# Images 3 and 4 convolved in 4x4 tiles, statistics as sums and squares on ScalarE, copies of the image in the linear attention

## The chip, the cores and the metric

One core of a Trainium2 chip runs the whole kernel. The metric is the device time of one execution in microseconds (us); the kernel before takes 3007.32 us (median of three runs, 3005.36 to 3007.85). All data are 32-bit floats. In the profile PE is TensorE, the matrix engine (PEld its weight loads), DVE is VectorE, ACT is ScalarE, POOL is GpSimd, and SP is the engine that issues most DMAs. Each of them works through its own list of instructions in the order written, and waits on semaphores where an operand or a buffer belongs to another.

## The reference

Four images of 256 channels and 64x64 pixels pass through four residual layers. Each layer first normalises its input by groups (`_gn`), so each needs the mean and variance of the whole image that the layer before it has just made.

```python
x = x + L0(_gn(x))   # 3x3 convolution, group norm, ReLU; non-local attention; 1x1; group norm
x = x + L1(_gn(x))   # RMS norm, linear attention in 4 heads, RMS norm
x = x + L2(_gn(x))   # dynamic depthwise 3x3 and pointwise convolution, kernels from pooled features
x = x + L3(_gn(x))   # mixture of 4 experts as one 1x1 convolution

# layer 0
xs = conv3x3(x, smooth_w) + smooth_b
xs = relu(group_norm(xs))                      # 8 groups
f  = einsum('bnc,bcm->bnm', theta_x, phi_x)    # 4096 x 4096 for each image
y  = einsum('bnm,bmc->bnc', softmax(f), g_x)
return group_norm(conv1x1(y, w_w)) * 0.1 + xs
```

## The kernel before

**Stages.** The image is kept as 128 partitions (channels of one half) by two halves by 4096 pixels. Image 1 is convolved alone (`convolve_first`) and projected to theta, phi and g (`project`). Then there is one stage for each image's non-local attention. `attend(b)` is a generator of 128 steps: a step multiplies 1024 columns of logits (`pf`, line 1021), takes their exponential on ScalarE (`pr`, line 1022), multiplies the step's probabilities with g (`py`, line 1129) and adds them up on VectorE (`tot`). The logits of a step are issued one step ahead of the products that use them. Every 16 steps a block of 512 rows ends, and its normalisation and output projection (`ended_by_dram`, lines 1038 to 1080) follow inside the next steps.

**What runs beside it.** `run(Chain(...).steps(), attention)` interleaves a second stream with these steps. The second stream is a generator that yields amounts of work; `Chain` multiplies them by a rate and lets one attention step go by for each whole unit (`steps`). `w.later(n, f)` puts a function n steps later. So a yield of 0.62 at a rate of 0.83 spaces the work by 0.51 attention steps. Beside the attention of image 1 (b = 0) run `scale_weights`, `filters_across` and `convolve_second`, at rate 1.33. Beside that of image 2 and of image 3 run `tail` of the image before and `convolve` of the image after, at rate 0.83. Beside image 4's runs the tail of image 3 at 1.2. After each stage comes `project`, which has the matrix engine to itself; the tail of image 4 is last and alone. Below, "stage 2" and "stage 3" are the attentions of images 2 and 3.

**The tail** of an image is `nonlocal_out` (normalise the attention's output, add it to the image; the sums of line 135 and statistics at line 1242), `linear_attention` (statistics at line 1431), `generated` (normalise, depthwise taps on VectorE, pointwise products on PE at line 1577, statistics at line 1591) and `mixed` (experts, line 1804).

**Two forms of the convolution.** Both turn the 3x3 convolution into products of transformed tiles, with the filters transformed once and kept in DRAM (`rows_d`, `filters`). `convolve` (images 3 and 4) makes 4x2 output tiles: 6x4 = 24 products for a tile, each product four matmuls of 512 columns, 96 matmuls in all. `convolve_second` (image 2) makes 4x4 output tiles: 36 products taken as 18 pairs, each pair eight matmuls of 256 columns, 144 matmuls in all (line 601). Its input is laid out by column phase (`planar`), written in `normalise_planar` (lines 661 on VectorE and 663 on ScalarE); `convolve` normalises in place (lines 670 and 672). Each product needs a tile `v` that VectorE makes from the row transform `ra` (`down` and `across`); the results are joined on VectorE from PSUM. A product's matmuls are put one step after its `v`. At the end the ReLU pieces run, two at once and the others inside `project`: one ScalarE instruction of 1024 columns for each piece after `convolve` (line 703), four of 256 columns with a re-ordering after `convolve_second` (line 698).

**Statistics.** They come from `bn_stats` on VectorE (512 columns at a time), except in the tail of image 4, where the pointwise result uses a sum taken by the adding instruction itself (line 1593) and squares on ScalarE with an accumulator (line 1595).

**Loads and copies.** The filter tiles `u` come through ScalarE's queue in `convolve` and through SP's in `convolve_second`. `copy_x` copies the raw image from DRAM to DRAM (`xs_d`) during the convolution. While `convolve` runs, the DMA that turns the row sums (`turning`, line 1054) goes through SP, else through ScalarE's queue.

## Time and profile before

The profiled execution took 3005.05 us, with a span of 3003.3 us from its first to its last instruction, so it lies 2 us under the median of the runs; 2 us of it lie outside the span.

| stretch of the span, us | what runs | length |
|---|---|---|
| 0 to 181 | image 1: convolution, projection | 181 |
| 181 to 744 | attention 1, convolution of image 2, projection | 563 |
| 744 to 1467 | attention 2, tail 1, convolution of image 3, projection | 723 |
| 1467 to 2190 | attention 3, tail 2, convolution of image 4, projection | 723 |
| 2190 to 2749 | attention 4, tail 3 | 559 |
| 2749 to 3003 | rest of attention 4, tail 4 | 255 |

A row of the group view reads: line, engine, operation, tiles written and read, partitions by elements, count, then busy time, mean duration of one in ns, and the engine's idle time before these instructions with what ended it. One matmul of the program is two matmul instructions in the profile (a 32-bit product is made in two passes), so the 96 matmuls of one image's convolution are 192 there and the 144 of the other form are 288. Instructions of one engine overlap at their ends: the spacing of two that follow each other is less than the duration of one.

### The profile page before, as it was taken

To read this page: it belongs to the slowest core of one execution; us is meant where nothing else is said; L and a number is where in the kernel's file an instruction comes from. 1 tells how busy PE (TensorE), PEld (TensorE's weight loads), DVE (VectorE), ACT (ScalarE), POOL (GpSimd) and SP (SyncE) were. 2 spreads that over 40 slices of the span, in tenths; PEclk is the share of its full clock that TensorE was granted. 3 is DMA by queue.
4 is the path that set the end of the run, shared out by engine and by line. 5 is a ranking of instruction groups with operands and counts; after the bars stand their busy time and mean duration, and the time that the engine had idled before them with its cause. 6 is when DMAs were issued, how large, how long until landed. Compare 5 with 4: busy or idle time off the path is not lost.

```text
span 3003.3 us, 25088 instructions
## 1 busy us (share of the span) xinstructions
PE 2953.0 (98%) x8750; PEld 1511.7 (50%) x8750; DVE 2058.4 (69%) x2835; ACT 1192.8 (40%) x2318; POOL 132.3 (4%) x182
## 2 busy tenths in 40 slices
PE   7999999999999999999999999999999999999998
PEld 3454555555565444444566444444546644444744
DVE  8747667773646994778455797578655468886585
ACT  2234333335456333322455533412335454333732
POOL 0000000001001000000001000000000100000100
PEclk9999999999999999999999999999999999999999
DMA  5245534224402225431610334243431222244021
GB/s 225 76 98 114 60 60 77 39 35 100 90 4 36 32 25 140 86 72 35 161 8 11 53 20 88 78 88 67 89 101 14 25 42 46 28 95 91 22 70 68
DMA packets 536133, 200.58 MB, mean 67 GB/s; under 512 B 471040, under 2 KB 481024, under 8 KB 532480
## 3 DMA queue, kind: packets, MB, share of 16 engines
q1 hardware_dynamic: 127808, 163.25, 17.6%
q10 hardware_dynamic: 403584, 18.88, 12.0%
q0 software_dynamic: 4608, 16.78, 3.7%
q8 instruction: 71, 1.16, 0.2%
q14 instruction: 62, 0.51, 0.1%
HBM read 130.13 MB, written 85.52 MB: 72 GB/s over the span
## 4 chain that ended last, share of the span: by engine, by line
PE 81%; DVE 12%; issue 5%; ACT 1%; POOL 0%; DMA 0%; DVEq 0%; POOLq 0%; ACTq 0%
PE pf L1021 25%; PE py L1129 24%; PE ps_conv L529 5%; PE ps_tp L957 4%; PE ps_qk L1303 3%; PE ps_ex L1804 3%; PE ps_pw L1577 3%; DVE tot L132 2%; DVE dw L135 2%; PE ps_conv L601 2%; PE ps_ctx L1330 2%; PE ps_g L962 2%; PE ps_o L1399 2%; PE ps_wy L1073 2%; PE ps_dw L1624 1%
## 5 line engine op out<-in xcount | busy, mean ns | idle before, releaser
L1022 ACT ACTIVATE pr<-pf 128x512 f32<-128x512 f32 x1024 | 603.1, 596 | 1092.0 <-PE pf L1021 1034.3
L1021 PE MATMUL pf<-tpg 128*128 128x512 f32 x2048 | 966.3, 594 | 0.0
L1129 PE MATMUL py<-pr,tpg 128*128 128x512 f32 x2048 | 961.7, 592 | 0.0
L132 DVE TENSOR_TENSOR tot<-tot,pr 128x1024 f32<-128x1024 f32 x448 | 546.5, 1220 | 181.8 <-ACT pr L1022 181.0
L1129 PEld LDWEIGHTS py<-pr,tpg 128*128 128x128 f32 x2048 | 389.2, 190 | 489.7 <-issue 481.6
L1021 PEld LDWEIGHTS pf<-tpg 128*128 128x128 f32 x2048 | 383.0, 190 | 428.4 <-issue 407.3
L135 DVE SCALAR_TENSOR_TENSOR dw<-xp,dk,dw 128x1008 f32<-128x1008 f32 x208 | 263.1, 1268 | 6.7 <-ACT dw L1569 3.6
L529 PE MATMUL ps_conv<-v,u 128*128 128x512 f32 x384 | 170.9, 593 | 3.2 <-DVE v L132 3.2
L132 DVE TENSOR_TENSOR tpg<-ps_g,bg_s 128x512 f32<-128x512 f32 x32 | 22.1, 692 | 146.9 <-PE ps_g L962 146.9
L529 PEld LDWEIGHTS ps_conv<-v,u 128*128 128x128 f32 x384 | 72.8, 190 | 95.8 <-issue 89.1
L957 PE MATMUL ps_tp<-big,wtpg_s 128*128 128x512 f32 x256 | 116.3, 594 | 2.7 <-ACT big L698 2.0
L225 POOL TENSOR_TENSOR rstd<-rstd,half 128x2 f32<-128x2 f32 x24 | 17.5, 729 | 2194.4 <-DVE rstd L382 2070.5
L1303 PE MATMUL ps_qk<-wqkv_s,xg 128*128 128x256 f32 x496 | 113.1, 379 | 0.0
L1303 PEld LDWEIGHTS ps_qk<-wqkv_s,xg 128*128 128x128 f32 x496 | 94.0, 190 | 21.3 <-issue 8.6
L1577 PE MATMUL ps_pw<-dw,pk 128*128 128x512 f32 x216 | 98.0, 593 | 0.9 <-DVE dw L135 0.9
L958 ACT ACTIVATE tpg<-ps_tp,btp_s 128x512 f32<-128x512 f32 x64 | 44.0, 687 | 95.3 <-PE ps_tp L957 95.3
L957 PEld LDWEIGHTS ps_tp<-big,wtpg_s 128*128 128x128 f32 x256 | 46.6, 190 | 54.5 <-issue 45.2
L1313 ACT ACTIVATE qk<-ps_qk,rinv 128x256 f32<-128x256 f32 x100 | 46.9, 474 | 65.2 <-PE ps_qk L1303 62.9
L962 PEld LDWEIGHTS ps_g<-wtpg_s,big 128*128 128x128 f32 x512 | 62.2, 192 | 15.3 <-issue 15.3
L132 DVE TENSOR_TENSOR v<-ra 128x1024 f32<-128x1024 f32 x58 | 69.2, 1221 | 0.3
L1812 ACT ACTIVATE res<-ps_ex,b 128x512 f32<-128x512 f32 x56 | 38.2, 687 | 76.0 <-PE ps_ex L1804 72.4
L1577 PEld LDWEIGHTS ps_pw<-dw,pk 128*128 128x128 f32 x216 | 40.9, 190 | 53.2 <-issue 49.7
(391 smaller groups left out, 3099.0 us busy)
## 6 DMA issues: line engine op xcount, KB each, us to landing
xp<-in_x_dram SPq DMA_DIRECT2D x16, 1024.0 KB, 8.1
xs_d<-big POOLq DMA_DIRECT2D x32, 512.0 KB, 6.4
wy_d<-wt SPq DMA_DIRECT2D x32, 512.0 KB, 2.8
wy<-wy_d SPq DMA_DIRECT2D x32, 512.0 KB, 4.0
out_dram<-res SPq DMA_DIRECT2D x64, 256.0 KB, 2.0
xs_d<-in_x_dram SPq DMA_DIRECT2D x24, 512.0 KB, 6.0
xs<-xs_d SPq DMA_DIRECT2D x24, 512.0 KB, 4.7
wp<-in_wp_dram SPq DMA_DIRECT2D x16, 512.0 KB, 5.3
```

The costliest lines, as they stand in the source:

```text
L132: nc.vector.tensor_tensor(o, a, b, op)
L135: nc.vector.scalar_tensor_tensor(o, a, s, b, op0, op1)
L529: nc.tensor.matmul(ps[oh], u(oh, h), v[:, bass.ts(h, 512)], start=(h == 0), stop=(h == NH - 1))
L601: nc.tensor.matmul(ps[:, bass.ts(oh, IY * IX)], u[i][:, h, bass.ts(oh, P)], v[:, i, bass.ts(h, IY * IX)], start=(h == 0), stop=(h == NH - 1))
L957: nc.tensor.matmul(ps, wtpg_s[:, h, k, :], big[:, h, cols], start=(h == 0), stop=(h == NH - 1))
L962: nc.tensor.matmul(ps[:, j, :], big[:, h, bass.ts(4 * c + j, P)], wtpg_s[:, h, 2, :], start=(h == 0), stop=(h == NH - 1))
L1021: nc.tensor.matmul(pf, phi[:, bass.ts(2 * m + s, P)], theta[:, bass.ts(q, 512)], start=True, stop=True)
L1022: nc.scalar.activation(pr[:, bass.ts(s, 512)], pf, AF.Exp)
L1129: nc.tensor.matmul(py, g[:, bass.ts(2 * m + s, P)], probs[i][:, bass.ts(s, 512)], start=(m == 0 and s == 0), stop=(m == NM - 1 and s == 1))
L1303: nc.tensor.matmul(ps[:, 0:2 * HID], xg[:, h, bass.ts(j, P)], wqkv_s[:, h, 0:2 * HID], start=(h == 0), stop=(h == NH - 1))
L1577: nc.tensor.matmul(ps, pk[:, h * NH * P + oh * P:h * NH * P + (oh + 1) * P], dw[h][:, bass.ts(s, 512)], start=(h == 0), stop=(h == NH - 1))
L1804: nc.tensor.matmul(ps, wm[h][:, bass.ts(oh, P)], big[:, h, bass.ts(c, 512)], start=(h == 0), stop=(h == NH - 1))
```

## The change

Images 3 and 4 are convolved by the same function as image 2, now called `convolve(w, b, pace)`. The old `convolve` is gone. The statistics of `nonlocal_out`, of the 4x4 convolution and of `generated` are taken as sums and squares: the sums by VectorE's adding instruction or by ScalarE, the squares by ScalarE. The last few lines of moments that this needs were in two places and are now two functions. `copy_x` for images 3 and 4 is issued in the linear attention's loop, and all filter tiles come through SP's queue.

```diff
+    def sums_tile():
+        return sp.tile([P, 2, NH, N // 512], F32, name="sums", bufs=1)
+    def joined_moments(st, sums, minus):
...
+    def accumulated(sums, pivot, parts=N // 512):
...
+    def load_filter_of(us, i, n):
+        if i < len(PRODUCTS):
+            a, pair = PRODUCTS[i]
+            k = pair[n]
+            u = filter_tile("u")
+            nc.sync.dma_start(out=u, in_=rows_d[...] if k in (0, 5) else filters[a, :, k - 1])
+            us.append(u)
@@ planar_joiner
+        def sums_of(n):
+            k, oh, s = 1 + n // 4, n // 2 % 2, n % 2
+            for i, f in enumerate((AF.Identity, AF.Square)):
+                nc.scalar.activation(junk()..., outs[:, oh, k, bass.ts(s, 2), :], f,
+                                     bias=minus[:, oh:oh + 1], accum_out=sums[...])
@@ input_stats
-                yield 0.3
+                yield 0.2
@@ normalise_planar
-            yield 1
+            yield 0.6
@@ normed_relu
-            if b == 1:
+            if b > 0:
@@ convolve
-    def convolve(w, b):
...
-    def convolve_second(w):
+    def convolve(w, b, pace):
+        us = []
+        if b > 1:
+            for n in range(2):
+                load_filter_of(us, 0, n)
         _, gm, rstd = yield from input_stats()
         yield from normalise_planar(gm, rstd)
...
-                for j in range(3):
-                    w.later(5 + j, lambda j=j: stats(j))
+                w.later(5, lambda: stats(0))
+                for j in range(8):
+                    w.later(6 + j, lambda j=j: sums_of(j))
...
-                pace = 1.8 if a == 5 else 0.87
+                slow = (2.07 if a == 5 else 1) * pace
                 for op, *args in down(a, planar, ra, rt, ra):
                     op(*args)
-                    yield 0.75 * pace
+                    yield 0.75 * slow
...
             for op, *args in ops:
                 op(*args)
-                yield 0.4 * pace
+                yield 0.4 * slow
             w.later(1, lambda ...: multiply(a, pair, v, u, after))
-            yield pace
+            yield slow
@@ ended_by_dram
-            turning[0].dma_start(...)
+            nc.scalar.dma_start(...)
...
             tt(yt, yt, inv, ALU.mult)
+            yield
             yield
@@ nonlocal_out
+        def squares(c, h):
+            for s in range(2):
+                nc.scalar.activation(junk(), big[:, h, bass.ts(2 * c + s, 512)], AF.Square, bias=about[:, h:h + 1],
+                                     accum_out=sums[:, 1, h, 2 * c + s:2 * c + s + 1])
         for i, (c, h) in enumerate(PARTS):
-            added(i, sc)
+            added(i, sc, accum_out=sums[:, 0, h, c:c + 1])
...
-            yield 0.7
-            for s in range(2):
-                nc.vector.bn_stats(st[:, h, 2 * c + s, :], big[:, h, bass.ts(2 * c + s, 512)])
-            yield 0.7
+            w.later(1, lambda c=c, h=h: squares(c, h))
+            yield 0.9
         w.settle()
+        yield from w.pending()
@@ linear_attention, loop over c
+            elif b + 2 < B and c % 2 == 0:
+                copy_x(b + 2, c // 2)
@@ generated, pointwise_added
-                    tt(big[:, oh, cols], res[oh], big[:, oh, cols], ALU.add)
-                    nc.vector.bn_stats(st[:, oh, c, :], big[:, oh, cols])
+                nc.vector.scalar_tensor_tensor(big[:, oh, cols], res[oh], 1.0, big[:, oh, cols], ..., accum_out=...)
+            def squares():
+                for oh in range(NH):
+                    nc.scalar.activation(junk(), big[:, oh, cols], AF.Square, bias=pivot[...], accum_out=...)
+            if diag is None:
+                w.later(1, squares)
@@ the stages
-            parts = [tail(b - 1, big, qT), lambda w: convolve(w, b + 1)] if b > 0 else [
-                scale_weights, filters_across, convolve_second]
+            parts = [tail(b - 1, big, qT), lambda w: convolve(w, b + 1, 0.53)] if b > 0 else [
+                scale_weights, filters_across, lambda w: convolve(w, 1, 0.87)]
-            run(Chain(both(*parts), 1.33 if b == 0 else 0.83).steps(), attention)
+            run(Chain(both(*parts), 1.365 if b == 0 else 0.775).steps(), attention)
-        run(Chain(tail(B - 2, big, qT, held=held), 1.2).steps(), attention)
+        run(Chain(tail(B - 2, big, qT, held=held), 1.225).steps(), attention)
```

By the order of the changed program, one image of stages 2 and 3 has its first convolution product in attention step 88 and its last in step 115, where it was 97 and 118. The tail is over, and `normalise_planar` runs, by step 84 to 87. In both programs the second stream ends within the 128 steps.

## The prediction

> **What bounds the kernel now.** I read first the page's span and busy times, which say that PE is busy for all but 50 us:

> ```profile
> span 3003.3 us, 25088 instructions
> ...
> PE 2953.0 (98%) x8750; PEld 1511.7 (50%) x8750; DVE 2058.4 (69%) x2835; ACT 1192.8 (40%) x2318; POOL 132.3 (4%) x182
> ```

> Next came windows by stage (PE, PEld, DVE, ACT, POOL busy, clock, DMA). The first two rows are stage 2, up to and from its first convolution product. The third is image 2's convolution, in the form that images 3 and 4 are to get. The last two are projections, after the old form and after the 4x4 form.

> ```profile
> 743.70:1230.50 486.80, 483.42 (x1435) 247.40 (x1434) 339.67 (x477) 218.95 (x449) 25.42 (x32) 1.00 0.28 53
> 1230.50:1390.00 159.50, 159.50 (x372) 70.78 (x373) 129.51 (x140) 34.89 (x59) 0.00 (x0) 1.00 0.39 73
> ...
> 329.00:670.00 341.00, 341.00 (x939) 178.14 (x939) 239.86 (x285) 109.60 (x185) 0.00 (x0) 1.00 0.36 57
> ...
> 1422.00:1466.80 44.80, 44.80 (x201) 27.79 (x200) 9.99 (x11) 19.54 (x26) 5.17 (x6) 1.00 0.69 142
> 696.00:743.70 47.70, 45.67 (x200) 27.50 (x199) 9.99 (x11) 27.74 (x44) 5.17 (x6) 1.00 0.63 127
> ```

> PE is full at clock 1.00, so PE work removed is time gained, as long as nothing makes PE wait. In 159.5 us of the old convolution VectorE has 30 us to spare. The 4x4 form of image 2 had 341 us for its VectorE work, and 101 to spare. The view of PE's waits over stage 2 shows how little it waits now:

> ```profile
> PE ps_conv L529 <- DVE v L132: 1.6, 1, 1.6
> PE ps_wy L1073 <- DVE yq L132: 1.1, 1, 1.1
> PE pm L364 <- DVE mv L132: 0.8, 2, 0.6
> ```

> The groups view prices the pieces:

> ```profile
> L529 PE MATMUL ps_conv<-v,u 128*128 128x512 f32 x384 | 170.9, 593 | 3.2 <-DVE v L132 3.2
> L601 PE MATMUL ps_conv<-v,u 128*128 128x256 f32 x288 | 65.1, 379 | 0.0
> L672 ACT ACTIVATE xp<-xp,nb,rstd 128x1024 f32<-128x1024 f32 x12 | 14.1, 1232 | 1.6 <-DVE nb L135 1.6
> L1595 ACT ACTIVATE junk<-tpg,pivot 128x512 f32<-128x512 f32 x16 | 11.6, 723 | 5.8 <-DVE tpg L1593 5.4
> L663 ACT ACTIVATE big<-xp,nb,rstd 128x1024 f32<-128x1024 f32 x4 | 9.1, 2286 | 2.4 <-DVE nb L135 2.4
> ```

> The timeline gives the spacing of instructions that follow each other, which is what counts where an engine is full:

> ```profile
> 668.92 2.35 DVE L132 TENSOR_TENSOR xp<-xp,rt 128x1024 f32<-128x1024 f32 x2
> ...
> 670.38 1.88 PE L1129 MATMUL py<-pr,tpg 128*128 128x512 f32 x4
> ...
> 672.10 1.88 PE L1021 MATMUL pf<-tpg 128*128 128x512 f32 x4
> ```
> ```profile
> 644.87 2.50 DVE L135 SCALAR_TENSOR_TENSOR rt<-sums 128x512 f32<-128x512 f32 x4
> ```
> ```profile
> 587.40 1.28 DVE L135 SCALAR_TENSOR_TENSOR ra<-big 128x1088 f32<-128x1088 f32 x1
> 588.60 1.22 DVE L132 TENSOR_TENSOR tot<-tot,pr 128x1024 f32<-128x1024 f32 x1
> ```

> Four matmuls of 512 columns take 1.72 us (0.43 each), so an attention step is 3.44 us of PE. On VectorE 512 elements cost (2.50-0.69)/3 = 0.60 us (0.69 is their duration alone), 1024 cost 2.35-1.22 = 1.13 and 1088 cost 1.20.

> **The change, part by part.** All terms are us in one execution.

> 1. *Matmuls.* Old, for one image: 170.9/2 = 85.4. New: 288 instructions, 65.1. Saved 20.3 an image, 40.7 for two. L601 costs 65.1/288 = 0.226 each against 170.9/384 = 0.445: half the columns, half the time. [...]

> 2. *The convolution against VectorE.* In the changed order, from first to last product of an image (28 steps), PE has 288 conv instructions (65.1), 216 of attention (0.43: 92.9) and 8 of output projection (3.4): 161. VectorE has 127 operations of 512 elements (76.2), 51 of 1024 (57.6), 20 of 1088 (24.0), small ones 2, and about 30 that read what the one before wrote, 0.1 more each: 163. The spare 30 us are gone: VectorE can't be ahead, each product's `v` becomes ready late, and behind it on PE wait the next logits, their exponentials and the next `tot`. At least the 2 us of excess and some 3 for the first `v`, which comes after the normalisation, are lost: 5. At most VectorE overlaps nothing: by full durations (0.69, 1.22, 1.285) its sum is 181, 20 more than PE, with the first `v` 23. VectorE must also wait for each product before it joins it, several short waits. I take 10, nearer the back-to-back rows, as VectorE will run back to back.

> 3. *Planar normalisation on ScalarE.* Four passes of L663 (2.29) take the place of four of L672 (1.23), in 2.4 x 0.775 = 1.9 steps, 6.4 us. ScalarE has 9.1 and two steps' exponentials (four of 0.6 overlapping, 2.2): 11.3, 4.9 too many. The exponentials wait in the queue behind the passes and `py` behind them; cover is the lead of one step. Range 0 to 5; I take 3.8. [...]

> 4. *Squares of `nonlocal_out`.* Sixteen of L1595's kind, 0.72 and some 0.13 for reading the accumulator (the 256-wide squares of L1285 last 0.38 and stand 0.51 apart): 13.6, within 8 x 0.9 x 0.775 = 5.6 steps or 19.2 us, beside 6.0 of exponentials: full. Each square waits for VectorE's addition, exponentials queue behind it. From 0 (one step's lead covers) to 7 (two pieces' four squares, 3.4, in a heap, twice): 4. The `bn_stats` saved on VectorE there (16 of 0.60) are off the path.

> 5. *Tail squeezed.* Rate 0.775 for 0.83: a tap (1.18 on VectorE) with its share of `tot` needs 1.18 + 0.48 x 1.13 = 1.72 in 0.62 x 0.775 = 0.48 steps, 1.65 of PE; it was 1.76 in 1.77. Over 64 taps VectorE falls 4.5 behind unless the pointwise products (64 instructions, 27.5) give it time. Other hand-overs in the tail lose cover alike. 0 to 10: 5. The pointwise statistics moved to ScalarE cost nothing there: by the first window it is busy 219 of 487.

> 6. *ReLU pieces.* The projection after the planar form is 47.7-44.8 = 2.9 longer: 2.9 an image (2 to 4).

> 7. *Removed waits:* 1.6 and about 0.9 of the others, -2.5.

> 8. *Stage 1.* `sums_of` (16 x 0.85) follows VectorE's joins for a = 4, exponentials queue behind: 0 to 5, taken 2.5. Last stages 0 (-2 to 2).

> 9. *DMAs.* SP's queue gets 36 filter loads an image and loses the turning DMA; ScalarE's loses 24 loads. A filter's second tile is loaded after the product before, 1.7 + 3.44 + 1.7 us ahead of use, and lands in 3.1 (median in the DMA view): hidden; 0. `copy_x` moves to another stretch with DMA share 0.28: 0.

> Sum: -40.7 + 2 x (10 + 3.8 + 4 + 5 + 2.9 - 2.5) + 2.5 = +8.2. On the profiled 3005.05 that is 3013.3; the median before is 2.3 above it: **3015**. The change breaks even where the stalls of a stage (25.7 here) come to 21.6.

> **The rivals.**

> *The cover holds.* Exponentials issued a step ahead and the buffers absorb all but 5 + 2.9 a stage: -40.7 + 2 x (7.9 - 2.5) = -29.9, 2977. For it: image 2's planar form in this trace made PE wait for nothing between 329 and 670. Against: there a product had 2.8 times the steps, and VectorE 101 us to spare. Half way to my stalls is 2996.

> *VectorE is the bound at full durations.* Term 2 at 23, the others as taken: +26 and +8.2 = +34, 3041. For it: dependent operations hardly overlap. Against: the back-to-back rows.

> *Filters late.* If SP's longer queue makes a tile land in 8 us rather than 3.1, 1.1 is lost in each of 36 products: +40, 3055. Against: stage 1 has this load order and no such wait.

> *It doesn't do what it says:* excluded for PE's work, since the changed order has 144 more matmuls of 256 columns in place of 96 for each image.

> **How the numbers follow.** 0.2% (6 us) is about what a measurement can tell from none. My forecast, stalls of 20 to 32 a stage, has 0.55: 0.39 slower, 0.15 within 6 us, 0.01 faster. The cover holds 0.25 (0.21 faster, 0.04 same). VectorE as bound 0.13, filters 0.07: slower but for 0.01. Together 0.22 faster, 0.20 same, 0.58 slower. My own case spans 3004 to 3028; the range reaches to 2988 and 3034, which leaves about 0.1 out on each side.

> **What would show it.** Conv matmuls of both stages near 130 us in all; PE's waits with ps_conv behind DVE `v`, about 10 in each of stages 2 and 3 and VectorE over 95% busy there; `py` behind ACT `pr` during the squares and the planar passes; projections of 47 to 48. I am wrong if PE waits less than 15 us a stage, or if its waits name a DMA.

## The result, and the profile after

The changed kernel takes 3029.24 us (median of four runs, 3025.12 to 3031.41) against 3007.26 (3005.36 to 3007.85): a ratio of 1.0073, 95% interval 1.0055 to 1.0090. It is 22 us slower. The profiled execution took 3028.17 us with a span of 3025.8.

The page's first lines:

```profile
span 3025.8 us, 26129 instructions
...
PE 2933.2 (97%) x8942; PEld 1558.0 (51%) x8942; DVE 2055.9 (68%) x2979; ACT 1330.3 (44%) x2654; POOL 131.6 (4%) x184
```

PE is busy 20 us less than before, half of what the matmuls were to save, and the span is 22.5 longer. Where: by the first logits of each attention, stage 1 grew from 562.6 to 565.2 us, stage 2 from 723.1 to 731.6, stage 3 from 723.1 to 733.5, and the rest from 813.3 to 813.8.

PE's waits in stage 2 (engine, line, what it waited for; us in all, times, longest):

```profile
PE ps_conv L658 <- issue: 7.2, 2, 4.5
PE py L1098 <- ACT pr L990: 7.1, 4, 3.1
PE ps_pw L1548 <- DVE dw L135: 2.5, 1, 2.5
PE ps_tp L927 <- ACT big L755: 2.0, 3, 0.7
PE ps_conv L658 <- DVE v L132: 1.8, 1, 1.8
PE ps_zt L1412 <- DVE zr L1389: 1.7, 2, 1.5
PE ps_b L1477 <- DVE w1n L132: 1.4, 1, 1.4
```

These are the stalls that were forecast, nearly to the microsecond: 9.0 for the convolution (the profile finds no releaser for two of its three waits and says "issue"), 7.1 for `py` behind ScalarE, and the tail's hand-overs. The longest "issue" ends as the first of VectorE's two operations on `v`, 0.69 long, does (start, length, engine, line, operation; in brackets the wait before it):

```profile
1369.02 1.41 DVE L135 SCALAR_TENSOR_TENSOR v<-v 128x512 f32<-128x512 f32 x2
1369.80 6.36 PE L658 MATMUL ps_conv<-v,u 128*128 128x256 f32 x16 [4.47 <-issue]
```

All of PE's idle time in stage 2 went from 4.0 to 24.8 us, in stage 3 from 4.1 to 26.0.

The surprise is in the column of the clock. Windows of the changed kernel, the stretch of the convolution and then five short ones around its longest wait (length, PE, PEld, DVE, ACT, POOL busy, granted clock, DMA share, GB/s):

```profile
1213.90:1388.00 174.10, 165.11 (x517) 100.87 (x516) 165.82 (x208) 46.58 (x81) 0.00 (x0) 0.97 0.35 65
```
```profile
1361.56:1364.97 3.41, 3.41 (x9) 1.33 (x7) 3.38 (x5) 1.78 (x3) 0.00 (x0) 1.00 0.00 0
1364.97:1368.38 3.41, 0.36 (x1) 0.00 (x0) 3.37 (x4) 0.00 (x0) 0.00 (x0) 1.00 0.44 84
1368.38:1371.80 3.42, 2.00 (x5) 1.67 (x6) 3.32 (x7) 0.00 (x0) 0.00 (x0) 0.50 1.30 37
1371.80:1375.21 3.41, 3.41 (x10) 2.69 (x9) 3.34 (x8) 0.60 (x1) 0.00 (x0) 0.50 1.87 28
1375.21:1378.62 3.41, 3.41 (x12) 1.87 (x11) 2.90 (x5) 1.30 (x3) 0.00 (x0) 1.00 1.00 84
```

PE does 0.36 us of work in the second window; in the next two its clock is 0.50, and then 1.00 again. VectorE is busy throughout, so it is the engine that PE waits for. In the kernel before, the clock was 1.00 in all of stages 2 and 3; here 27.3 us of them lie at 0.50, each time at or just after one of the longest waits. The convolution's matmul instructions follow each other at 0.427 us there (the median of 37) and at 0.216 elsewhere. PE is busy 25.2 of these 27.3 us, so 12.6 us are lost to it. This is the part that the prediction lacks.

### The profile page after: what moved, and what is told of

It is laid out like the page before. It is cut to its first block, busy times and chain, and to the rows that moved or that the text cites. A ratio compares the mean times of both kernels' runs of the same rounds, so it can differ in the third digit from the quotient of the medians.

```text
span 3025.8 us, 26129 instructions
## 1 busy us (share of the span) xinstructions
PE 2933.2 (97%) x8942; PEld 1558.0 (51%) x8942; DVE 2055.9 (68%) x2979; ACT 1330.3 (44%) x2654; POOL 131.6 (4%) x184
## 3 DMA queue, kind: packets, MB, share of 16 engines
q8 instruction: 72, 1.18, 0.2%
## 4 chain that ended last, share of the span: by engine, by line
PE 85%; DVE 8%; ACT 3%; issue 2%; DMA 1%; POOL 0%; SPq 0%; DVEq 0%; POOLq 0%; ACTq 0%
PE pf L989 26%; PE py L1098 26%; PE ps_conv L658 6%; PE ps_tp L927 3%; PE ps_qk L1284 3%; PE ps_pw L1548 3%; PE ps_ex L1779 3%; PE ps_ctx L1311 2%; PE ps_wy L1042 1%; PE ps_dw L1599 1%; PE ps_row L611 1%; PE ps_conv L572 1%; PE ps_g L932 1%; PE ps_o L1382 1%; DVE dw L135 1%
## 5 line engine op out<-in xcount | busy, mean ns | idle before, releaser
L132 DVE TENSOR_TENSOR tot<-tot,pr 128x1024 f32<-128x1024 f32 x448 | 546.7, 1220 | 191.0 <-ACT pr L990 189.7
L135 DVE SCALAR_TENSOR_TENSOR dw<-xp,dk,dw 128x1008 f32<-128x1008 f32 x208 | 263.1, 1269 | 6.7 <-ACT dw L1540 3.6
L658 PE MATMUL ps_conv<-v,u 128*128 128x256 f32 x864 | 205.0, 392 | 19.2 <-issue 14.4
L658 PEld LDWEIGHTS ps_conv<-v,u 128*128 128x128 f32 x864 | 170.0, 197 | 69.6 <-issue 36.7
L132 DVE TENSOR_TENSOR tpg<-ps_g,bg_s 128x512 f32<-128x512 f32 x32 | 22.1, 692 | 153.1 <-PE ps_g L932 153.1
L135 DVE SCALAR_TENSOR_TENSOR sums<-ps_conv,sums 128x512 f32<-128x512 f32 x72 | 49.7, 690 | 51.1 <-PE ps_conv L658 49.9
L663 ACT ACTIVATE sums<-ps_conv 128x512 f32<-128x512 f32 x36 | 21.5, 598 | 118.1 <-PE ps_conv L658 118.1
L1787 ACT ACTIVATE res<-ps_ex,b 128x512 f32<-128x512 f32 x56 | 38.2, 688 | 73.4 <-PE ps_ex L1779 70.6
```

What stands on the lines that cost most here:

```text
L132: nc.vector.tensor_tensor(o, a, b, op)
L135: nc.vector.scalar_tensor_tensor(o, a, s, b, op0, op1)
L658: nc.tensor.matmul(ps[:, bass.ts(oh, IY * IX)], u[i][:, h, bass.ts(oh, P)], v[:, i, bass.ts(h, IY * IX)], start=(h == 0), stop=(h == NH - 1))
```

## The experiments

**1. Filling the waits** (stall and clock told apart).

```diff
+    def busy(ps, n):
+        for i in range(n):
+            nc.tensor.matmul(ps[:, 0:P], ones, ident, start=(i == 0), stop=(i == n - 1))
@@ multiply, logits, pointwise_products (stages 2 and 3)
+    busy(...)   # 5, 9, 17 before three products; 11 before one pair of logits; 8 before one pointwise product
```

> The changed kernel, and besides in each of stages 2 and 3 short matmuls that no result depends on (ones by the identity, 128 columns, some 0.22 us each; their bank is overwritten at once by the product behind them), put on PE just ahead of the five longest waits: 11 (2.4 us) where the planar normalisation makes `py` wait 3.1, 5 (1.1) in the convolution's wait of 1.8, 9 (2.0) in that of 2.7, 17 (3.7) in that of 4.5, 8 (1.7) in the pointwise products' wait of 2.5. The waits' ends are set by ScalarE and VectorE, so the fillers lie inside them. Theory (half clock): PE runs at half speed for 3.4 or 6.8 us after a wait that left it idle for most of a 3.4 us window; 27.3 us at 0.5 in stages 2 and 3 cost half of that, 13.7. With the fillers these rows of 0.5 are gone and the time is 3029.2 - 13.7 = 3015.5 (3012 to 3018), with the same waits of ps_conv, py and ps_pw less the fillers. Rival (the waits are all of it; the recorded half clock costs nothing, or comes from something else than idle time): 3029 (3027 to 3032), or the rows of 0.5 stay.

Measured: 3018.62 us (3017.09 to 3019.11), ratio to before 1.0039 (1.0026 to 1.0053): 10.6 less than the changed kernel, by adding work, and 0.6 above the range of the theory. Only one window at half clock is left in stages 2 and 3 (behind the squares of stage 3, which had no filler). PE's waits in stage 2:

```profile
PE py L1106 <- ACT pr L998: 4.7, 4, 2.2
PE ps_conv L664 <- DVE v L132: 2.9, 4, 1.2
...
PE ps_pw L1558 <- DVE dw L135: 0.7, 1, 0.7
```

The same waits, less the fillers. Half of the busy time at half clock fell from 12.6 to 1.7, so 10.9 were to be had (the 13.7 of the theory counted the windows' whole length, and all of them); stages 2 and 3 became 9.4 shorter and the span 10.9. The rival falls.

**2. What triggers the half clock.** The kernel before, with waits of set length in stage 1.

```diff
+            if b == 0 and i in IDLE:          # every 7 steps, 1 to 7 copies, twice
+                t = junk()
+                for s in range(2):
+                    ps = bank("ps_idle")
+                    nc.tensor.matmul(ps, ones, theta[:, 0:512] if s == 0 else t, start=True, stop=True)
+                    for j in range(IDLE[i] if s == 0 else 0):
+                        nc.scalar.copy(t, ps if j == 0 else t)
```

> The kernel before with 14 waits put into the attention of stage 1, where PE is full: every 7 steps one matmul, a chain of 1 to 7 ScalarE copies of 512 columns (some 0.5 us each) that starts from its result, and a matmul that reads the chain's end; nothing uses the results. PE is idle some 0.8 to 4.5 us each time, twice for each length. Theory (a free-running grid of windows of 3.413 us; one in which PE is idle for more than about 0.6 halves the clock of the next): waits under 2 us are never followed by 0.5, waits over 4.1 always, and between them it goes by the share of the window and not by the length: every window above 0.65 idle is followed by 0.5, none below 0.55; all starts of 0.5 lie on one grid of 3.413 us. Rival (the length of the wait decides, from about 2.5 us): waits of 2.5 to 4 are all followed by 0.5, wherever they fall.

Measured (one execution, 3091.72 us): waits of 0.68, 1.38 and 1.98 us were never followed by 0.50; those of 3.01, 3.27, 3.98 and 4.57 always. Two waits of nearly one length went different ways. Windows on the grid around the wait that ended at 339.8 (2.68 us) and around that at 593.0 (2.63 us):

```profile
334.53:337.94 3.41, 2.57 (x6) 0.78 (x5) 2.79 (x4) 1.91 (x4) 0.00 (x0) 1.00 0.57 107
337.94:341.35 3.41, 1.58 (x4) 0.86 (x5) 0.19 (x1) 1.72 (x3) 0.00 (x0) 1.00 0.06 22
341.35:344.77 3.42, 3.42 (x9) 1.51 (x9) 0.00 (x0) 1.00 (x2) 0.00 (x0) 1.00 0.00 0
...
590.53:593.95 3.42, 0.94 (x2) 0.49 (x3) 2.03 (x2) 2.34 (x4) 0.00 (x0) 1.00 0.00 0
593.95:597.36 3.41, 3.41 (x5) 1.35 (x4) 0.00 (x0) 0.00 (x0) 0.00 (x0) 0.50 0.00 0
597.36:600.77 3.41, 3.41 (x9) 1.52 (x8) 0.83 (x1) 1.19 (x2) 0.00 (x0) 1.00 0.00 0
```

**3. Spacing the planar normalisation.**

```diff
-            yield 0.6
+            yield 0.6 if b == 1 else 1.2
```

> The changed kernel with 1.2 in place of 0.6 between the four quarters of the planar normalisation of images 3 and 4 (1.9 attention steps more for it, and the convolution two steps later). Theory: four passes of 2.25 us then share 3.7 steps with the exponentials and fit; the 3.1 us wait of `py` falls to 1.5 or less, and with it one halved window, so at least 2 x (1.6 + 1.7) = 6.6 go: 3022.6, and less, down to 3005, if the convolution's waits of 2.7 and 4.5 (which fall differently against the ends of the blocks of 16 steps) come under 2 us too and their halved windows go as well. Rival (the wait only moves: VectorE is full behind it anyway, and what the normalisation gives is lost in the convolution): 3027 to 3031.

Measured: 3011.29 us (3008.55 to 3013.35), ratio 1.0016 (1.0007 to 1.0025), 18 less than the changed kernel. The wait of `py` fell from 3.1 to 1.0; the convolution's waits of 2.7 and 4.5 became 1.6, 1.3 and 1.6, and the windows at 0.50 there are gone. That lies between the two values expected, and the rival falls: PE's idle time in the two stages went from 50.8 to 41.7.

**4. VectorE's load in the convolution.**

```diff
-            elif m > 1:
+            elif m > 1 and not (b in (1, 2) and 88 <= i < 116):
                 tt(tot, tot, probs[i], ALU.add)
```

> The changed kernel without VectorE's `tot` additions in steps 88 to 115 of stages 2 and 3 (26 additions of 1024 columns a stage, 29 us; the row sums are then short of these steps). Theory (the convolution's waits come from a full VectorE that brings `v` late): with 29 us less of 166 VectorE is ahead, the conv waits of 9.0 and 11.2 us fall under 2 a stage, the halved windows behind them (10.2 us of 0.5 a stage) go; those of the normalisation stay: 3029.2 - 2 x (8 + 5) = 3003 (2999 to 3008). Rival (the waits are the way from a product over its joining to the next `v`, not VectorE's load): conv waits stay above 5 a stage, 3018 or more.

Measured: 2999.73 us (2996.79 to 3002.05). The stretch of stage 2's convolution, columns as above:

```profile
1215.70:1373.80 158.10, 158.10 (x513) 97.14 (x512) 138.38 (x183) 45.95 (x80) 0.00 (x0) 1.00 0.37 72
```

With 138 us of VectorE's work in 158 PE waits for nothing, where it waited 9.0 with 166 in 174. The convolution's waits are VectorE's load, as term 2 had it, and not the way from product to join to next `v`.

**5. The two halves of the change apart.** The changed kernel with the statistics of the attention's output and of the pointwise result taken as before:

```diff
-            w.later(1, lambda c=c, h=h: squares(c, h))
-            yield 0.9
+            yield 0.7
+            for s in range(2):
+                nc.vector.bn_stats(st[:, h, 2 * c + s, :], big[:, h, bass.ts(2 * c + s, 512)])
+            yield 0.7
@@ pointwise_added: bn_stats on VectorE in place of the sums and squares, in the same way
```

> The changed kernel with the statistics of the attention's output and of the pointwise result from bn_stats on VectorE again, as before the change (the loop of the former with its two amounts of 0.7, so the tail is three steps longer); the 4x4 form and its own sums stay. Theory (waits by their sizes, and half clock): the waits of `py` behind the squares, 1.05 + 2.2 a stage, go, so -6.5: 3022.7; the later convolution may change its waits and halved windows, 3010 to 3027. Rival (VectorE takes the place: 16 passes of 0.6 us a stage come back to it, and the tail at rate 0.775 has no room): 3029 or more.

And the kernel before with these statistics taken as in the changed one, nothing else:

> The kernel before with nothing but the new statistics of the attention's output and of the pointwise result (sums by the adding instruction, squares on ScalarE), at its own rate of 0.83 and with the 4x2 form. Theory: the squares in a heap make `py` wait 1.05 + 2.2 us a stage as in the changed kernel, the small waits change little, and no wait reaches the length that halves the clock: 3007.3 + 2 x 3.3 = 3014 (3010 to 3017). Rival (ScalarE is 45% busy and hides them; the waits in the changed kernel come from its faster tail): 3007, within 3.

Measured: 3014.12 us (3012.41 to 3015.61), ratio 1.0025 (1.0014 to 1.0035), and 3020.11 us (3015.33 to 3023.16), ratio 1.0041 (1.0027 to 1.0055). So each half makes the kernel slower, by 7 and by 13. That this adds up to 20 of the 22 is no proof that the halves are independent, since each moves the other's waits. PE's waits in stage 2 of the first kernel:

```profile
PE ps_pw L1548 <- DVE dw L135: 4.4, 2, 3.4
PE ps_conv L658 <- DVE v L132: 4.2, 3, 2.3
```

Without the squares the waits of `py` behind them went, as expected, and the convolution, three steps later, waited 1.1, 0.8 and 2.3 for 1.8, 2.7 and 4.5; the wait for the pointwise taps grew from 2.5 to 3.4. The second expectation was too low by 6. Stage 3 of the second kernel:

```profile
PE py L1168 <- ACT pr L1061: 3.3, 2, 2.2
PE ps_conv L568 <- DMA u<-rows_d: 2.8, 1, 2.8
PE ps_ex L1847 <- DVE wm L132: 1.7, 1, 1.7
PE ps_b L1545 <- DVE w1n L132: 1.4, 1, 1.4
```

The squares cost the 3.3 foreseen; the faster tail (0.9 for 1.4 a part) moved other hand-overs, and two windows were at half clock. Which of these the three steps did alone was not tried.

**6. Filters on ScalarE's queue, copies during the convolution** (term 9): together, then each alone.

```diff
-            nc.sync.dma_start(out=u, in_=...)
+            (nc.scalar if b > 1 else nc.sync).dma_start(out=u, in_=...)     # both, filters
-            if b == 1 and i % 3 == 2 and i < 12:
+            if i % 3 == 2 and i < 12:                                       # both, copies
                 copy_x(b, i // 3)
@@ linear_attention, loop over c
-            elif b + 2 < B and c % 2 == 0:                                  # both, copies
-                copy_x(b + 2, c // 2)
```

> The changed kernel with the filter tiles of images 3 and 4 through ScalarE's queue and the copies of the image during the convolution again. Theory (DMAs cost nothing here, term 9): 3029 within 4, and the waits of PE name no filter. Rival (SP's longer queue or the copies in the tail cost some of the missing 14 us): 3015 to 3024.

> The changed kernel with the filter tiles of images 3 and 4 through ScalarE's queue; the copies stay in the linear attention. Of the 23 us that both together cost, theory (the second tile's load is issued behind ScalarE's reading of the product before, `sums` from ps_conv, and behind exponentials that wait for PE, so PE waits for the tile, then ScalarE for PE): all of it, 3052 (3047 to 3055), with waits of ps_conv that name DMA u. Rival (the copies take the DMA engines or SP from the filters): 3029 within 4.

> The changed kernel with the copies of the image during the convolution again, eight of 512 KB an image on SP's queue among the filter loads; the filters stay on SP's queue. Theory (copies are hidden in either place): 3029 within 4. Rival (eight copies of some 6 us each ahead of filter tiles that land in 3 us make tiles late): 3035 to 3052.

Measured: 3052.28 us (3049.99 to 3053.32), 3033.35 (3030.48 to 3035.31) and 3033.29 (3032.18 to 3034.02). Together they cost 23 us, where neither side expected a loss over 4. Each alone costs some 4 by the medians, where the runs of the changed kernel spread over 6.3. My theory for the filters was wrong, and for the copies neither side holds. The kernel with both, PE's waits in stage 2, and the issues of SP and ScalarE with the product that waits (start, length, engine, line, operation; q is the engine's queue):

```profile
PE ps_conv L659 <- DMA u<-filters: 5.4, 2, 4.0
PE ps_conv L659 <- DMA u<-rows_d: 3.8, 1, 3.8
```
```profile
1212.67 1.19 SPq L737 DMA_DIRECT2D xs_d<-in_x_dram  x2
1215.17 1.27 SPq L737 DMA_DIRECT2D xs_d<-in_x_dram  x2
...
1217.07 5.49 ACTq L539 DMA_DIRECT2D u<-filters  x2
...
1226.22 2.57 PE L659 MATMUL ps_conv<-v,u 128*128 128x256 f32 x8 [4.03 <-DMA u<-filters]
1268.92 2.42 SPq L737 DMA_DIRECT2D xs_d<-in_x_dram  x4
```

And SP's copies in the kernel with the copies alone:

```profile
1223.45 1.20 SPq L736 DMA_DIRECT2D xs_d<-in_x_dram  x2
1255.07 1.20 SPq L736 DMA_DIRECT2D xs_d<-in_x_dram  x2
1278.95 1.27 SPq L736 DMA_DIRECT2D xs_d<-in_x_dram  x2
1308.55 1.19 SPq L736 DMA_DIRECT2D xs_d<-in_x_dram  x2
```

With the filters in the same queue the copies go out in pairs of 512 KB, 24 to 32 us apart, because SP stops for each tile's buffer (between 1213 and 1330 us it waits 23 times for a product to free one, 89 us in all). Without them SP runs ahead and sends four within 4 us. The tile issued at 1217.07, just behind four, landed 9.0 us later and is used at 1226.22; the median landing of such tiles in the whole run is 2.7. It was not issued later than in the changed kernel (1217.58 there), so "behind ScalarE's reading" was not the cause. With the filters alone PE was idle no longer than in the changed kernel (50.1 against 50.8); those 4 us come with more windows at half clock (41.0 us against 27.3).

**7. Pacing.** Four amounts of the changed kernel altered:

```diff
-            run(Chain(both(*parts), 1.365 if b == 0 else 0.775).steps(), attention)
+            run(Chain(both(*parts), 1.365 if b == 0 else 0.76).steps(), attention)
-  convolve(w, b + 1, 0.53)
+  convolve(w, b + 1, 0.55)
-            yield 0.6      # normalise_planar
+            yield 0.9
-            yield 0.9      # nonlocal_out
+            yield 1.2
```

> The changed kernel with four amounts altered and nothing else: the rate of stages 2 and 3 0.76 for 0.775, the pace of their convolution 0.55 for 0.53, 0.9 for 0.6 between the quarters of the planar normalisation, 1.2 for 0.9 between the parts of the attention's output. Theory (the loss is waits where ScalarE or VectorE has a heap of work, and the half clock behind the longest of them): the squares get 1.33 times the steps (the waits of 3.3 a stage fall to 1.5), the normalisation 1.5 times (3.1 falls to 2 or less), the convolution's products lie a little further apart, and no wait reaches 2.3, so no window is halved: 3029.2 - 13.7 - 2 x (1.8 + 1.1 + 2 to 6) = 2998 to 3006, below the kernel before. Rival (VectorE has no room for it: what is taken from one part of the 128 steps is missed in another): 3009 to 3020, like the spaced normalisation alone (3011.3) or worse.

Measured: 2992.42 us (2991.27 to 2993.07), ratio to before 0.9951 (0.9938 to 0.9965). It is faster than both kernels, by 14 and 37 us, and 6 below the range expected: PE's idle time in the two stages fell by 23.6, where some 10 to 18 were expected. Of the 37, 1.9 lie in stage 1, whose normalisation has the same amount.

```profile
span 2990.5 us, 26125 instructions
...
PE 2921.4 (98%) x8942; PEld 1547.6 (52%) x8942; DVE 2054.9 (69%) x2979; ACT 1327.6 (44%) x2654; POOL 128.6 (4%) x184
```
```profile
PE py L1098 <- ACT pr L990: 3.7, 5, 1.6
PE ps_tp L927 <- ACT big L755: 2.0, 3, 0.7
PE ps_zt L1412 <- DVE z L132: 1.5, 1, 1.5
PE ps_b L1477 <- DVE w1n L132: 1.4, 1, 1.4
PE ps_conv L658 <- DVE v L132: 1.4, 1, 1.4
```

No wait of stages 2 and 3 is over 1.6 us (ps_zt, ps_b and the ReLU pieces stay as they were), and none of their windows is at half clock. The work is that of the changed kernel. The same amounts, with bn_stats again:

> The kernel with the four altered amounts (2992.4), but the statistics of the attention's output and of the pointwise result by bn_stats on VectorE, in the same steps (0.6 and 0.6 in place of 1.2). Theory (statistics on ScalarE are worth something where steps are short): a part of the output then needs 1.13 + 2 x 0.60 and 0.91 of a `tot` (1.0) of VectorE, 3.4 us, in 0.91 steps, 3.1 of PE, so VectorE falls some 2 us behind a stage, the waits of `py` behind the squares (1.0 to 1.6) go, and the pointwise additions get 8 us more of VectorE: 2 x (2 to 6) slower, 2996 to 3004. Rival (they only move work from one idle engine to another): 2992 within 3; or faster, as the unpaced kernel was without them (3014 against 3029).

Measured: 3026.33 us (3024.82 to 3029.21), ratio 1.0064 (1.0050 to 1.0078): 34 us slower, far more than the 4 to 12 expected, and the rival is wrong by its sign. VectorE is late everywhere behind the place (stage 2):

```profile
PE ps_pw L1548 <- DVE dw L135: 4.9, 2, 3.8
PE py L1098 <- ACT pr L990: 2.9, 4, 1.1
PE pm L403 <- DVE mv L132: 2.9, 1, 2.9
PE ps_conv L658 <- DVE v L135: 2.8, 3, 1.6
PE ps_conv L658 <- issue: 2.3, 1, 2.3
```

and 17.1 us are at half clock. So statistics on ScalarE cost 13 us in the kernel before and 15 in the changed one (in both together with the shorter amounts of 0.9 for 1.4 a part), and are worth 34 in the paced one, at equal amounts.

**The account of all of them.** For stages 2 and 3 together, in the profiled executions: what is left of the length after PE's idle time and half of its busy time at clock 0.50 should be PE's work at full clock, the same in every kernel of one form.

| kernel | length | PE idle | lost to half clock | rest |
|---|---|---|---|---|
| before | 1446.2 | 8.0 | 0 | 1438.2 |
| statistics alone (4x2) | 1461.5 | 18.8 | 3.2 | 1439.5 |
| changed | 1465.1 | 50.8 | 12.6 | 1401.7 |
| spaced normalisation | 1448.5 | 41.7 | 3.4 | 1403.4 |
| old statistics | 1448.2 | 38.2 | 6.8 | 1403.2 |
| no `tot` in the convolution | 1437.2 | 30.5 | 6.8 | 1399.9 |
| queues, both | 1485.8 | 63.1 | 20.1 | 1402.6 |
| filters on ScalarE | 1470.5 | 50.1 | 18.8 | 1401.6 |
| copies in the convolution | 1469.7 | 54.3 | 13.3 | 1402.1 |
| paced | 1431.9 | 27.2 | 0 | 1404.7 |
| paced, old statistics | 1463.8 | 48.8 | 8.4 | 1406.6 |

It is: 1438 to 1440 for the old form, 1400 to 1407 for the 4x4 form. The kernel with filled waits (1455.7, 29.2, 1.7) leaves 1424.8, of which its 200 filler instructions are 22 at 0.11 each: 1403. Three numbers, work, idle time and half clock, account for every kernel to some 4 us.

## Why the prediction was right and wrong

The side was right (slower, 0.58) and the time, 3015, was 14 us too low, inside the range of 2988 to 3034. By its terms:

- *Matmuls (1).* Right: the old products follow each other at 0.429 us an instruction, the new at 0.216, so the saving by these is 2 x (192 x 0.429 - 288 x 0.216) = 40.3, against 40.7. The account shows 1438.2 - 1401.7 = 36.5 of it, because each wait also brings to light the end of the matmul before it: one of 512 columns lasts 0.594 and the next starts after 0.429, and 21 more waits (31 of over 0.15 us in the two stages, against 10) at 0.165 are 3.5.
- *Convolution against VectorE (2).* Right: 10 forecast, 9.0 and 10.2 measured, VectorE at 95%; experiment 4 shows the cause.
- *Planar normalisation (3).* Right: 3.8 forecast, 3.1 measured. L720 took 2.25 us a pass, near the 2.29 of image 2's row. The passes of the old layout took 1.232 (L672), those of the new layout nearly twice as long.
- *Squares (4).* Right: 4 forecast, 4.2 measured with the `pm` behind them.
- *Tail (5).* Right in size: 5 forecast, 6.2 measured; the largest, 2.5, is the first pointwise product's wait for its taps.
- *ReLU pieces (6).* 2.9 forecast, 2.0 of idle time measured.
- *Removed waits (7).* 2.5 forecast; of the 4.0 a stage before, the 2.7 of `ps_conv` and `ps_wy` are gone, and what is left of the rest is counted in terms 4 and 5.
- *Stage 1 and the rest (8).* 2.5 forecast, 2.7 and 0.5 measured.
- *DMAs (9).* Right for the change: no long wait names one. But the cover was thinner than I said. Without the two moves the same form would cost 23 us more (experiment 6).

Together PE's idle time in stages 2 and 3 grew by 42.8, and with the 3.5 of matmul ends by 46.3, where the terms have 46.4. Single terms were off by up to 1.2 a stage, so it is luck that the sum is this close.

What failed is the sentence under the first view: "PE is full at clock 1.00, so PE work removed is time gained, as long as nothing makes PE wait." The clock of 1.00 belonged to a kernel whose PE never waited longer than 1.6 us in these stages. I priced each wait at its length and carried the clock over, so the sum has no term for it. I forecast sums of waits and thought of short ones; four a stage come in one piece of 2.5 to 4.5 us, and six of these eight are followed by 3.4 or 6.8 us at half speed: 12.6 us. With the term the sum is 8.2 + 12.6 = 20.8, against 22.5 by the spans. In the six windows of 3.413 us just ahead of those at half speed PE was idle for 0.66 to 1.00 of each, so not always throughout.

Of the rivals, "the cover holds" fell with the first view of the waits. "VectorE at full durations" lies, at 3041, about as far above the measured time as mine lies below it, and its mechanism is not the one seen: the convolution's waits were 9 and 10, not 23. "Filters late" is real where the copies share the stretch, and wasn't in this change.

## What to carry to other kernels

In these traces a wait of the matrix engine between full stretches cost its length alone only while it was short: in experiment 2 none of 0.68 to 1.98 us was followed by half clock; in stages 2 and 3 of the changed kernel four of the eight of 2.2 to 3.1 us were, and both of 4.5. So one heap of work spread over two more steps was worth more than its own wait (experiment 3: 18 us, 9.1 of them idle time). The statistics moved here from one engine with time to spare to another brought nothing but a loss until the pace was set again for what they free; the same change lost 22 us with one set of four amounts and gained 14 with another. Before a removed piece of work is booked as gain, ask which clock, and which cover, the new idle time will take away.

## What the hardware showed that I had not expected

- Over the profiles of the twelve kernels other than that of before, between 185 and 2750 us, every window of the 3.413 us grid at clock 1.00 in which PE was idle for 0.59 or more was followed by 0.50 (the lowest 0.59, twice), and none with 0.57 or less was (the highest 0.57, three times). In the changed kernel's the six that were followed had 0.66 to 1.00, and the highest of the others 0.55. In the first convolution and the last tail, windows with 0.37 to 0.57 were followed too; that stays open.
- Where a wait ran on into the halved window, the clock stayed at 0.50 for a second one: such windows were idle for 0.19 to 0.67 (0.41 and 0.19 in the changed kernel; 6.83 us at 0.50 each time, so a loss of up to 3.4).
- A share of 0.59 is 2.0 us of a window of 3.413, and a wait that the grid cuts in two halves would need 4.0 (an estimate from these two numbers). By it, the place in the grid sets whether a wait between the two costs 1.7 us more, half of 3.413. The squares' wait of 2.2 us, the same in eight of the kernels profiled, was caught in stage 2 or 3 of seven of them, and not in the changed kernel's profile. The runs of the changed kernel spread over 6.3 us, those of the paced one over 1.8; that the grid does it fits, but was only argued.
- SP's waits paced what it issued behind them: with the filter loads taken out of its queue, four copies of 512 KB went out within 4 us in place of pairs 24 to 32 us apart (experiment 6), and a tile behind the four came after 9.0 us, where the median is 2.7.
